# A recurrent layer with a gated residual: the gate's second layer in four steps instead of eight, and each later stage begun earlier

## The chip, the cores and the metric

The kernel runs on one core of one Trainium2 chip. The metric is the device time of one execution in microseconds; 3016.45 us is the median of three runs (3016.45, 3016.9 and 3013.8). The profile is that of one further execution.

## What is computed

64 sequences of 256 steps, 1024 wide, all in fp32. The first layer is a recurrence, and the second one adds its input to a gated reconstruction of it:

```python
xW  = einsum('ntd,dh->nth', x, Wx) + b
h_t = tanh(h_{t-1} @ Wh + xW_t)             # h_{-1} = cond
x1  = x + h
h   = silu(cond @ W1.T + b1)
gate = sigmoid(h @ W2.T + b2)               # one row per sequence
y   = x1 + (x1 + inverse_haar(gate * haar(x1)))
```

The gate is the same for all coefficients of a sequence, so the transform and its inverse cancel, and `y = x1 * (2 + gate)`. The kernel calls `2 + gate` its `factor`. It needs the two layers of the gate once, and before the first output is scaled.

## The kernel before

**The products.** `h @ Wh` has to be done step by step. It is 64 x 1024 x 1024 in fp32, done as one level of Strassen's scheme: seven products of half size (`strassen_product`, L212), each of 16 matmuls 128x32 x 128x128 on four strips of TensorE. `x Wx` doesn't wait for the recurrence. It is done for two steps at a time, 128 rows, a "pair" n holding steps 2n and 2n + 1. To keep precision with the fast fp32r matmuls, x and Wx are split in pieces: 24 matmuls 128x128 x 128x512 go to each 512 columns, 8 to a bank `mixed` and 16 to a bank `main`, 48 in all (`XWork`, L291). The sum of both banks goes to DRAM and comes back in the layout of h (`sum_d`, `xw`). ACT copies the reloaded `xw` into the accumulators of the next step (`put`, `put_part`).

**The stages.** There are four, and `ALONE`, `SWITCH` and `FIRST` say where they part.

- Single steps, t = 0 to `ALONE` - 1 (L526 to L602; `ALONE` = 12). After each h product comes half an x product: `XWork.first` after odd steps (`mixed`, and the first third of `main`), `XWork.second` after even ones. From t = 3 (`LATE`) on, each step also loads one of eight blocks of W2 (512 KB each, L588) and multiplies it with the gate's hidden layer `g1T` (`plain_product`, L229, 16 matmul records per block). This gate product stands last in the step, after the half x product. After the eighth block `gate_factor` (L499) makes `factor`. Pairs that are finished before `factor` is there are put aside in DRAM (`kept`, L597). At the end of a pair the x of the pair three further on is loaded (`load_x`).
- Pairs of steps, t = `ALONE` to `SWITCH` - 1 (`SWITCH` = 22). Two h products follow each other, in a form that works by quarters of h (L1080 to L1131), and then one whole x product (`beside_x`, `XWork.whole`). The first of these whole products comes ahead of step `ALONE`. `kept_pair` (L698) reads a pair that was put aside, scales it and stores it.
- Pairs after the switch (`beside_two`, kind "plain"; seven pair numbers lie between `SWITCH // S` and `FIRST`). The same 48 matmuls, but other buffers: x is loaded a second time by steps (`r`), and the slabs of the first stages are given up (`switch`, L726). In these pairs the weights for the last stage are formed (`make_forms`).
- Units of two pairs, from pair `FIRST` = 18 on (kinds "one" for even and "two" for odd n). Six of the eight row blocks of Wx are done as before; the last two are done by Strassen's scheme over two pairs. A unit has 54 + 39 = 93 matmuls of 512 columns where two plain pairs have 96.

**What sets the order.** TensorE's order is the order in which the program is written, everywhere. DVE's and ACT's order is written out in the start-up and from step `ALONE` on; in the single steps between, a scheduler chooses it, and that of POOL and SP as well. All transfers but one are issued by SP, in order, so an issue that waits holds back what stands behind it. In the stages from `ALONE` on, `not_ahead_of` (L644) lets the store of the sums wait for an instruction late in the h products. `slab` tiles (six buffers of 512 KB) hold x, the blocks of W2 and the pairs that are read again; a load waits until the last reader of an old slab is done.

`nc.tensor.addr_align(256, 60)` near the end of an x product (L360, L1009) pads TensorE's instructions, so that what follows stands at a given place within a block of 256.

Of the kernel before, what the change touches and what calls it, by code (L numbers as in the profile page):

```python
# [53 lines left out]
F32 = mybir.dt.float32  # L54
# [6 lines left out]
N, T, D = 64, 256, 1024  # L61
P = 128
R = 32
Q = P // R
B = D // P
# [5 lines left out]
S = 2  # L71
# [6 lines left out]
WARM = 6  # L78
LATE = 3
AHEAD = 2  # L80
ALONE = LATE + B + 1
RINGS = 1024
BLOCK = 256
PLACE = 60
SWITCH = 22
FIRST = SWITCH // S + 7
FULL = B - 2
EVEN = 16
# [3 lines left out]
def tile_cond_resid(  # L92
# [16 lines left out]
    nc = tc.nc  # L109
# [5 lines left out]
    dram = ctx.enter_context(tc.tile_pool(name="dram", bufs=2, space=bass.MemoryType.DRAM))  # L115
# [13 lines left out]
    def slab(name: str):  # L129
        return slabs.tile([P, D], F32, tag="slab", name=name)  # L130
# [91 lines left out]
    def plain_product(ps, vT, w, k: int, of=None, start: bool = True, stop: bool = True) -> None:  # L222

        for g in range(G):
            col = of(g) if of else (g * B + k) * R
            for q in range(Q):


                nc.tensor.matmul(  # L229
                    out=ps[q * R : (q + 1) * R, g * F : (g + 1) * F],  # L230
                    lhsT=vT[:, col : col + R],
                    rhs=w[:, q * F : (q + 1) * F],
                    start=start and k == 0 and g == 0,
                    stop=stop and k == B - 1,
                    skip_group_check=True,
                    tile_position=(0, q * R),
                )

    def strassen_sides(hT, t: int):
        a11, a12, a21, a22 = (hT[:, i * E : (i + 1) * E] for i in range(4))  # L240
        s = sums.tile([P, 4, E], F32, tag="s", name=f"s{t}")
        nc.vector.tensor_add(s[:, 0], a21, a22)
        nc.vector.tensor_sub(s[:, 2], a11, a21)
        nc.vector.tensor_sub(s[:, 1], s[:, 0], a11)
        nc.vector.tensor_sub(s[:, 3], a12, s[:, 1])
        return {1: a11, 2: a12, 3: s[:, 3], 4: a22, 5: s[:, 0], 6: s[:, 1], 7: s[:, 2]}
# [4 lines left out]
    def put(xw, t: int):  # L251

        acc = bank("acc", f"acc{t}")
        nc.scalar.copy(acc, flat(xw))
        return acc
# [30 lines left out]
    def bank(tag: str, name: str):  # L286
        return one_pool.tile([P, HALF], F32, tag=tag, name=name)
# [165 lines left out]
    acc, acc1, gate_ps = bank("acc", "acc0"), bank("m57", "acc1_raw"), bank("gate", "gate_ps1")  # L453
# [17 lines left out]
    def gate_block(k: int) -> None:  # L471
        plain_product(gate_ps, h0T, w1[k], k)

    for k in range(B):
        x_block(k)
        split_block(k)
        if k == 0:
            now = XWork(1)
# [20 lines left out]
    def gate_factor(z):  # L499

        nc.vector.tensor_add(z, gate_ps, z)
        nc.scalar.activation(z, z, AF.Sigmoid)
        factor = const.tile([P, W], F32, tag="factor", name="factor")
        nc.vector.transpose(factor, z)
        nc.vector.tensor_scalar_add(factor, factor, 2.0)
        return factor

    def blocks(v):
        return v[:].rearrange("p (g b m) -> p g b m", g=G, b=B)
# [5 lines left out]
    def of_step(x, s: int):  # L515
        return x[:].rearrange("p (b s g m) -> p s g b m", b=B, s=S, g=G)[:, s]
# [4 lines left out]
    h = work.tile([P, W], F32, tag="h", bufs=1, name="h0")  # L521
    nc.vector.tensor_add(h, acc, b_n)


    kept, again, factor = [], [], None
    for t in range(ALONE):  # L526
        i, s = divmod(t, S)
        if s == 0 and t:
            xw = xw_next
        if t:  # L530
            h = h_product(acc, sides, t)
        hT = work.tile([P, W], F32, tag="hT", name=f"hT{t}")
        nc.scalar.activation(h, h, AF.Tanh)
        nc.vector.transpose(hT, h)
        sides = strassen_sides(hT, t)
        if t == 0:
            acc = bank("acc", "acc1")
            nc.vector.tensor_add(acc, acc1, b_n)
            for k in range(2, B):
                if k == B - 1:  # L540
                    for j in range(4):
                        gate_block(j)
                now.block(k)
            now.take_mixed()
            for k in range(4, B - 2):
                gate_block(k)
            later = XWork(2)
            wh_s = StrassenWeight(wh_raw)
            wh_s.first()
            wh_s.second()  # L550
            wh_s.third()
            wh_s.fourth()
            xw_next = now.finish()
            later.split()

        elif s == 0:
            acc = put(xw[1], t + 1)
            now.second()
            later = XWork(i + 2)
            later.split()  # L560
            xw_next = now.finish()
        if s == 1 and t + 1 < ALONE:
            now = later
            now.first()
            acc = put(xw_next[0], t + 1)

        if t == 1:
            in_order.close()
        if t == 2:
            g1T = gate_hidden(b1_n)  # L570
            b2_n = load_bias(b2, const, "h0T", "b2_n")


        x = pairs[i]
        if t == 0:
            hT0 = hT
        elif t == 1:

            for r, v in enumerate((hT0, hT)):
                tc.keep_in_program_order(nc.gpsimd.tensor_add(of_step(x, r), of_step(x, r), blocks(v)))  # L580
        elif t + 1 < ALONE:
            nc.gpsimd.tensor_add(of_step(x, s), of_step(x, s), blocks(hT))
        if LATE <= t < LATE + B:
            k = t - LATE
            if k == 0:
                gate_ps = bank("gate", "gate_ps2")
            w2 = slab(f"w2_{k}")
            nc.sync.dma_start(out=w2, in_=w2T[k])  # L588
            plain_product(gate_ps, g1T, w2, k)
            if k == B - 1:  # L590
                factor = gate_factor(b2_n)
        if t + 1 == ALONE:
            break
        if factor is not None:
            scale(x, s)
        elif s == S - 1:
            kept.append(dram.tile([P, D], F32, tag="kept", bufs=(LATE + B) // S, name=f"kept{i}"))  # L597
            nc.sync.dma_start(out=kept[i], in_=x)
        if s == S - 1:
            del pairs[i]  # L600
        if s == S - 1 or t + 2 == ALONE:
            load_x(i + 3)  # L602
# [20 lines left out]
    )  # L623
    xws = {ALONE // S: xw_next}

# [15 lines left out]
        v = x_step(t)  # L641
        nc.vector.tensor_add(v, v, blocks(hT))

    def not_ahead_of(dma, ins) -> None:  # L644
        tc.add_manual_dep(
            dma.ins,
            ins.ins.name,
            mybir.DependencyInfo(mybir.DependencyClass.Sync, mybir.DependencyReason.DATA),
            reason="transfers stay out of the products of h",
        )  # L650

    def store_y(i: int) -> None:
        nc.sync.dma_start(out=yT[i], in_=pairs.pop(i))

# [16 lines left out]
    def beside_x(t: int, later, now, scaled: list, mark):  # L671


        if later:
            d, dma = later.store()
            not_ahead_of(dma, mark)
        load_next()
        if later:
            xws[later.i] = later.reload(d, True)
        now.whole(True)  # L680
        residual(t, hT)
        for r in scaled:
            scale(pairs[r // S], r % S)
        now.take_mixed()
        if mark:
            accs[:] = [put_part(t + 1, j) for j in range(3)]
        nxt = XWork(now.i + 1)
        nxt.difference()
        nxt.low()
        now.finish_half(0)  # L690
        now.finish_half(1)
        kept_pair()
        store_done(t)
        return now, nxt

    again = []
# [22 lines left out]
    def store_step(t: int) -> None:  # L719
        nc.sync.dma_start(out=yS[t - SWITCH], in_=steps.pop(t))  # L720

    def load_step(t: int):
        steps[t] = new["pool"].tile([P, W], F32, tag="r", bufs=3, name=f"r{t}")
        return nc.sync.dma_start(out=steps[t], in_=xS[t - SWITCH])

# [119 lines left out]
    def beside_two(t: int, now, mark):  # L845
# [4 lines left out]
        n = now.i  # L850
        start_of = t + 1 == SWITCH
        kind = "plain" if n < FIRST else "one" if n % 2 == 0 else "two"
# [152 lines left out]
        for k, (out, lhs, rhs, start) in enumerate(todo):  # L1005
            for do in at.get(k, []):
                do()
            if k == len(todo) - 2 or kind == "two" and k == len(todo) - 2 - EVEN:
                nc.tensor.addr_align(BLOCK, PLACE - (3 * EVEN if k < len(todo) - 2 else 0))  # L1009
            if k == 1 and kind == "plain" and i in (SWITCH // S + 2, SWITCH // S + 3):  # L1010
                next(jobs[0])
# [11 lines left out]
        if kind == "plain":  # L1023
            jobs[0] = jobs[0] or make_forms()
            next(jobs[0], None) if i not in (SWITCH // S + 2, SWITCH // S + 3) else None
        if with_next:
# [23 lines left out]
    for t in range(ALONE, T):  # L1050
        i, s = divmod(t, S)
# [6 lines left out]
        h = work.tile([P, W], F32, tag="h", bufs=1, name=f"h{t}")  # L1058
        hT = None if final else work.tile([P, W], F32, tag="hT", name=f"hT{t}")
# [46 lines left out]
        mark = nc.scalar.copy(u, m16)  # L1106
# [80 lines left out]
```

## Time and profile before

| | us |
|---|---|
| median of three runs | 3016.45 |
| the profiled execution's own time | 3014.26 |
| its span, first to last instruction | 3012.5 |
| TensorE busy (matmuls) | 2999.2 |
| DVE busy | 2210.5 |
| POOL busy | 967.1 |
| ACT busy | 913.8 |

In the span, step 3 (the first one with a gate block) has its h product at 71.27, the single steps end at 181.88 with the start of the first whole x product, the pairs of steps run from 193.03, the h product after the switch begins at 310.36, and the first unit's x product at 443.67.

How to read the lines that follow later: in a timeline the first column is the start in us from the span's start, the second the time from the start of the first to the end of the last instruction of the merged group, then engine, source line, operation, output <- inputs, shapes, count. Matmuls are pipelined, and a group's end overlaps the start of the next one, so the length of a piece is taken as the difference of two starts. A bracket at the end tells how long the engine idled ahead of the group and what ended it; "issue" means that nothing in the profile was waited for. `m`, `m_h`, `main_h` and `acc` are banks of the h products, `gate_ps` that of the gate. The queue q8 carries TensorE's instructions, q1 the kernel's transfers.

### The profile page before, as it was taken

The page shows a single profiled execution, that of the slowest core. Times are in us where ns is not written, and L with a number is a line of the kernel's source. Part 1 is how long each engine was busy: PE and PEld are TensorE (multiplying, and loading weights), DVE is VectorE, ACT ScalarE, POOL GpSimd, SP SyncE. Part 2 cuts the span into 40 slices and gives each one's busy share as a digit, 9 for nine tenths or more (in the row PEclk, how much of TensorE's full clock was granted, in tenths as well). Part 3 has the DMA queues.
Part 4 walks back from the last instruction along what each step waited for, and adds up shares of the span by engine and source line. Part 5 has one row for each costly group of instructions (what it writes and reads, how often), then busy time and mean ns, then how long its engine had stood idle before and what let it go on. Part 6 is the DMA issues. An engine that isn't in the chain of part 4 may idle for free.

```text
span 3012.5 us, 147059 instructions
## 1 busy us (share of the span) xinstructions
PE 2999.2 (100%) x63697; PEld 2674.8 (89%) x63697; DVE 2210.5 (73%) x5594; ACT 913.8 (30%) x2753; POOL 967.1 (32%) x800
## 2 busy tenths in 40 slices
PE   9999999999999999999999999999999999999999
PEld 6888888998898889988988889889988998899888
DVE  7555667777777777777777777777777777777776
ACT  3222232322333233223332232233332322333222
POOL 2233333333333333333333333333333323333331
PEclk9999999999999999999999999999999999999999
DMA  7334454444544544445445444454454444544543
GB/s 266 115 114 135 156 179 157 142 149 151 170 143 142 171 157 141 150 153 167 143 142 170 158 141 146 153 171 143 141 172 157 141 149 152 170 143 143 172 155 111
DMA packets 263546, 461.99 MB, mean 153 GB/s; under 512 B 30080, under 2 KB 103552, under 8 KB 262912
## 3 DMA queue, kind: packets, MB, share of 16 engines
q1 hardware_dynamic: 262768, 452.06, 46.6%
q8 instruction: 514, 8.42, 1.1%
q14 instruction: 120, 0.98, 0.1%
q10 hardware_dynamic: 144, 0.52, 0.0%
HBM read 313.00 MB, written 139.46 MB: 150 GB/s over the span
## 4 chain that ended last, share of the span: by engine, by line
PE 97%; DMA 1%; POOL 0%; SPq 0%; issue 0%; DVE 0%; ACT 0%; DVEq 0%; POOLq 0%
PE main L890 23%; PE acc L212 22%; PE m_h L212 15%; PE main_h L212 14%; PE mixed L890 12%; PE chain_main L890 3%; PE main L291 3%; PE chain_mixed L890 2%; PE mixed L291 1%; PE m L212 1%; PE acc L229 1%; DMA xw<-sum_r 0%; PE gate_ps L229 0%; DMA x<-xT 0%; SPq L793 0%; POOL sum L337 0%
## 5 line engine op out<-in xcount | busy, mean ns | idle before, releaser
L890 PE MATMUL main<-wx,x 128*128 128x512 f32 x3052 | 746.4, 389 | 0.0
L871 POOL TENSOR_TENSOR r<-r,factor 128x512 f32<-128x512 f32 x230 | 318.7, 1386 | 1282.7 <-DVE r L639 998.1
L890 PEld LDWEIGHTS main<-wx,x 128*128 128x128 f32 x3052 | 572.8, 188 | 119.2
L786 POOL TENSOR_TENSOR xw<-xw,b_h 128x512 f32<-128x512 f32 x230 | 384.9, 1680 | 328.5 <-DMA xw<-sum_r 275.3
L1063 ACT ACTIVATE h<-h 128x128 f32<-128x128 f32 x976 | 275.5, 306 | 522.8 <-DVE h L1089 312.8
L890 PE MATMUL mixed<-wx,x 128*128 128x512 f32 x1526 | 389.0, 399 | 0.0
L632 ACT COPY acc<-xw 128x128 f32<-128x128 f32 x726 | 184.9, 267 | 554.9 <-POOL xw L786 460.1
L890 PEld LDWEIGHTS mixed<-wx,x 128*128 128x128 f32 x1526 | 277.4, 188 | 76.5 <-issue 23.0
L1067 DVE STREAM_TRANSPOSE hT<-h 128x128 f32<-128x128 f32 x972 | 298.1, 307 | 41.6 <-ACT h L1063 39.5
L212 PE MATMUL acc<-t,hT 128*32 128x128 f32 x8160 | 270.8, 273 | 2.1 <-issue 1.2
L212 PE MATMUL acc<-wh,s 128*32 128x128 f32 x8160 | 271.4, 273 | 1.5 <-issue 1.5
L212 PE MATMUL acc<-wh,hT 128*32 128x128 f32 x8160 | 269.7, 273 | 0.0
L212 PE MATMUL m_h<-wh,hT 128*32 128x128 f32 x7808 | 261.0, 274 | 1.7 <-ACT u L1106 1.7
L212 PE MATMUL main_h<-t,s 128*32 128x128 f32 x7808 | 260.6, 273 | 0.6 <-issue 0.5
L212 PE MATMUL main_h<-wh,s 128*32 128x128 f32 x7808 | 258.8, 273 | 0.0
L212 PE MATMUL m_h<-t,s 128*32 128x128 f32 x7808 | 258.8, 273 | 0.0
L807 ACT ACTIVATE sum<-chain_mixed 128x512 f32<-128x512 f32 x220 | 131.7, 598 | 399.0 <-PE chain_mixed L890 343.7
L212 PEld LDWEIGHTS m_h<-wh,hT 128*32 128x32 f32 x7808 | 208.2, 110 | 44.6 <-DVE sum L810 18.3
L212 PEld LDWEIGHTS acc<-t,hT 128*32 128x32 f32 x8160 | 227.5, 110 | 5.2 <-ACT acc L632 1.9
L212 PEld LDWEIGHTS acc<-wh,s 128*32 128x32 f32 x8160 | 229.6, 110 | 1.8 <-issue 1.7
L212 PEld LDWEIGHTS acc<-wh,hT 128*32 128x32 f32 x8160 | 227.9, 110 | 0.3
L315 DVE TENSOR_TENSOR x<-x,x_high 128x1024 fp32r<-128x1024 f32 x127 | 215.7, 1699 | 9.3 <-PE main L291 9.3
(135 smaller groups left out, 4074.0 us busy)
## 6 DMA issues: line engine op xcount, KB each, us to landing
wx<-form SPq DMA_DIRECT2D x330, 256.0 KB, 6.3
x<-xT SPq DMA_DIRECT2D x128, 512.0 KB, 4.2
sum_r<-sum SPq DMA_DIRECT2D x468, 128.0 KB, 2.2
r<-xS SPq DMA_DIRECT2D x233, 256.0 KB, 5.8
yS<-r SPq DMA_DIRECT2D x233, 256.0 KB, 6.0
xw<-sum_r SPq DMA_DIRECT2D x232, 256.0 KB, 4.9
ahead<-xT SPq DMA_DIRECT2D x55, 128.0 KB, 4.6
sum_d<-sum SPq DMA_DIRECT2D x10, 512.0 KB, 2.9
```

The lines of the kernel that those rows point to most:

```text
L212: nc.tensor.matmul(out=out[q * R : (q + 1) * R], lhsT=a[:, k * R : (k + 1) * R], rhs=wh_s.sides[i][k][:, q], start=first and k == 0, stop= ...
L229: nc.tensor.matmul(out=ps[q * R : (q + 1) * R, g * F : (g + 1) * F], lhsT=vT[:, col : col + R], rhs=w[:, q * F : (q + 1) * F], start=start ...
L291: nc.tensor.matmul(out=acc[h], lhsT=v[:, k * P : (k + 1) * P], rhs=wx_s[k][which][:, h * HALF : (h + 1) * HALF], start=start and k == 0, s ...
L315: nc.vector.tensor_sub(self.x1, x, self.high)
L632: nc.scalar.copy(part, xws[t // S][t % S][:, j])
L786: nc.gpsimd.tensor_add(v, v, new["b"][:].unsqueeze(1).broadcast_to((P, G, F)))
L807: nc.scalar.activation(out, mixed, AF.Copy, scale=-1.0)
L871: nc.gpsimd.tensor_mul(steps[r], steps[r], factor)
L890: nc.tensor.matmul(out=out, lhsT=lhs, rhs=rhs, start=start, stop=stop, skip_group_check=True)
L1063: nc.scalar.activation(quad(h, j), quad(h, j), AF.Tanh)
L1067: nc.vector.transpose(quad(hT, j), quad(h, j))
```

## The change

The gate's second layer takes two blocks per step (`EACH = 2`), in steps 3 to 6. Its products are issued right after the h product and ahead of the half x product, and both loads of W2 of step t wait for the transpose of h of step t - 1. So `ALONE` goes from 12 to 8, `SWITCH` from 22 to 14 and `FIRST` from 18 to 14; three pairs are put aside instead of five. `not_ahead_of` is only moved up. The first whole x product is no longer padded.

```diff
+EACH = 2
-ALONE = LATE + B + 1
+ALONE = LATE + B // EACH + 1
-SWITCH = 22
+SWITCH = 14
 FIRST = SWITCH // S + 7
...
-    kept, again, factor = [], [], None
+    def not_ahead_of(dma, ins) -> None:
+        tc.add_manual_dep(
+            dma.ins,
+            ins.ins.name,
...
+        )
+
+    kept, again, factor, turned = [], [], None, []
     for t in range(ALONE):
...
-        nc.vector.transpose(hT, h)
+        turned.append(nc.vector.transpose(hT, h))
         sides = strassen_sides(hT, t)
+        for k in range((t - LATE) * EACH, (t - LATE + 1) * EACH) if LATE <= t < LATE + B // EACH else []:
+            if k == 0:
+                gate_ps = bank("gate", "gate_ps2")
+            w2 = slab(f"w2_{k}")
+            not_ahead_of(nc.sync.dma_start(out=w2, in_=w2T[k]), turned[t - 1])
+            plain_product(gate_ps, g1T, w2, k)
...
-        if LATE <= t < LATE + B:
-            k = t - LATE
-            if k == 0:
-                gate_ps = bank("gate", "gate_ps2")
-            w2 = slab(f"w2_{k}")
-            nc.sync.dma_start(out=w2, in_=w2T[k])
-            plain_product(gate_ps, g1T, w2, k)
-            if k == B - 1:
-                factor = gate_factor(b2_n)
+        if t == LATE + B // EACH - 1:
+            factor = gate_factor(b2_n)
...
-            kept.append(dram.tile([P, D], F32, tag="kept", bufs=(LATE + B) // S, name=f"kept{i}"))
+            kept.append(dram.tile([P, D], F32, tag="kept", bufs=(LATE + B // EACH) // S, name=f"kept{i}"))
...
-        now.whole(True)
+        now.whole(mark is not None)
```

More of the change, by code (lines that the diff above doesn't have):

```diff
@@ L522, in tile_cond_resid @@
     nc.vector.tensor_add(h, acc, b_n)
-    kept, again, factor = [], [], None
+    def not_ahead_of(dma, ins) -> None:
+        tc.add_manual_dep(
+            dma.ins,
+            ins.ins.name,
+            mybir.DependencyInfo(mybir.DependencyClass.Sync, mybir.DependencyReason.DATA),
+            reason="transfers stay out of the products of h",
+        )
+    kept, again, factor, turned = [], [], None, []
     for t in range(ALONE):
@@ L642, in residual @@
         nc.vector.tensor_add(v, v, blocks(hT))
[L644 to L650, printed above, removed]
     def store_y(i: int) -> None:
```

## The prediction

> **What bounds the kernel.** I read the page first: the busy table, the chain that ended last, and the queue table.
>
> ```profile
> span 3012.5 us, 147059 instructions
> PE 2999.2 (100%) x63697; PEld 2674.8 (89%) x63697; DVE 2210.5 (73%) x5594; ACT 913.8 (30%) x2753; POOL 967.1 (32%) x800
> ...
> q8 instruction: 514, 8.42, 1.1%
> ...
> PE 97%; DMA 1%; POOL 0%; SPq 0%; issue 0%; DVE 0%; ACT 0%; DVEq 0%; POOLq 0%
> ```
>
> TensorE is busy for the whole span and is 97% of the chain. So the time is a sum of TensorE pieces that follow each other, and an edit is worth what it takes out of, or puts into, that sum. POOL, DVE and ACT have room. Secondly I read TensorE's timeline to get the length of each piece. One single step (step 6, and the start of step 7):
>
> ```profile
> 111.56 1.06 PE L212 MATMUL m<-wh,hT 128*32 128x128 f32 x32
> ...
> 117.78 5.78 PE L291 MATMUL main<-wx,x 128*128 128x512 f32 x24
> 123.49 1.07 PE L229 MATMUL gate_ps<-w,g1T 128*32 128x256 f32 x16
> 124.38 1.06 PE L212 MATMUL m<-wh,hT 128*32 128x128 f32 x32
> ```
>
> Differences of the first column: h product 117.78 - 111.56 = 6.22, half an x product 5.71, one gate block 0.89, in all 12.82 us. One pair of steps, in the stage after it, and one unit of two pairs, later:
>
> ```profile
> 216.49 1.08 PE L212 MATMUL m_h<-wh,hT 128*32 128x128 f32 x32
> ...
> 239.96 1.08 PE L212 MATMUL m_h<-wh,hT 128*32 128x128 f32 x32
> ...
> 549.48 1.08 PE L212 MATMUL m_h<-wh,hT 128*32 128x128 f32 x32
> ...
> 595.73 1.08 PE L212 MATMUL m_h<-wh,hT 128*32 128x128 f32 x32
> ```
>
> A pair is 23.47 us and a unit of two pairs 46.25 (the next one 46.26). The windows view of these stretches shows TensorE busy in all of them at a granted clock of 1.00. A plain pair after the switch is 23.47 too (336.30 to 359.77). Thirdly, the places where the pieces are longer than that. In step 4:
>
> ```profile
> 84.07 1.06 PE L212 MATMUL m<-wh,hT 128*32 128x128 f32 x32
> ...
> 88.44 0.61 PE L212 MATMUL acc<-t,hT 128*32 128x128 f32 x12
> 89.97 0.74 PE L212 MATMUL acc<-t,hT 128*32 128x128 f32 x18 [0.93 <-issue]
> ...
> 91.62 5.73 PE L291 MATMUL main<-wx,x 128*128 128x512 f32 x24
> ```
>
> Here the h product takes 7.55 us instead of 6.22, and TensorE waits for "issue", that is for no tile. In step 5 it takes 6.86. Steps 6 to 11 show none of it. What it waits for is its own instructions: counted in the built program (an fp32 matmul as two weight loads and two matmuls, padding included) TensorE has 131,665 instructions, 514.3 times 256, and q8 carried 514 packets of 16 KB. In an h product 448 instructions pass in 6.22 us, so 256 last 3.56 us. In step 4 a block's packet began at 87.03, took 1.24, and TensorE went on at 89.97; meanwhile the queue of SP had issued, in the middle of it, a block of w2 (84.23) and an x load (84.67), and the DMA moved 340 to 430 GB/s from 85.8 to 87.9.
>
> ```profile
> 84.23 0.35 SPq L588 DMA_DIRECT2D w<-w2T  x1
> 84.67 0.38 SPq L134 DMA_DIRECT2D x<-xT  x1
> 98.22 0.33 SPq L403 DMA_DIRECT2D sum_d<-sum  x1
> 98.64 0.38 SPq L588 DMA_DIRECT2D w<-w2T  x1
> ```
>
> So a stall needs two things: a block asked for early in an h product, and a data transfer under way just then.
>
> **The change, part by part.** (1) *Steps 8 to 11 become two pairs, and x products 5 and 6 whole ones.* Four steps without gate are 4 x (6.22 + 5.71) = 47.72; two pairs 2 x 23.47 = 46.94. Gain 0.8.
>
> (2) *Gate.* The count of matmuls stays. Eight pieces of 0.89 (7.1) become four of two blocks; a run of 32 gate matmuls in the start-up takes 43.30 to 45.05 = 1.75, so 7.0. Gain 0.1.
>
> (3) *Units from pair 14 instead of 18.* Pairs 14 to 17 cost 4 x 23.47 = 93.88 now and 2 x 46.25 = 92.50 as units. Gain 1.4. The built order agrees: 36 plain x matmuls less and 30 for the units more, 6 fewer, at 0.227 us each 1.36.
>
> (4) *The switch at step 14.* Pairs 7 to 10 go from whole products to plain ones, 23.47 against 23.47: nothing. The h product just after the switch shows 14.84 us against 12.36 (310.36 to 325.20; loads of 2.2 MB are issued from 307.43 on). The same transfers are issued in the same order at the new place, and the alignment puts the h product at place 64 of a block as before, so I carry these 2.5 us over unchanged, and likewise the 1.9 us of smaller stalls in the pieces from 359.77 to 503.01.
>
> (5) *Two pairs less are put aside and read again* (kept, again): DMA alone, nothing on TensorE.
>
> (6) *The w2 loads.* Their new wait for the transpose of the step before holds SP's queue. In step 2 hT is done at 67.97, where SP issued w2_0 at 66.90: 1.1 later. Queued behind it are w2_1, the load of x4, the store of the sums and the reload of xw4. The store waits for DVE till 72.2 anyhow; xw4 was consumed by ACT's copy at 81.17 and is needed by the second product of step 4 at 84.94 (85.8 in the new plan): 3.8 us of cover. x4 lands about 2 later than 72.9, but then the 76.2 of g1T comes first on DVE; y of step 3 moves from 76.19 to about 76.9, behind which lie 7.4 us of gate and x on TensorE. g1T is there at 76.26 and the first gate block is due at 77.52. The landing of w2 took 3.4 to 5.8 us here: issued at 68.5, w2_1 is there by 74.3, cover 3 us. In step 3 w2_2 and w2_3 go behind kept (81.50) at about 82, landed by 88 and due at 91.2. In step 4 w2_4, w2_5 and x5 wait for hT4 (about 94) and for the slabs that the gate of step 4 reads till 93. x5 went out at 84.67 and now goes at 95, landing by 100.5; DVE's mask of it stands ahead of y of step 5, due at 103: cover 2.5, and behind it the 7.4 of gate and x again. w2_7 follows kept2, which waits for POOL (1.4 us): issued by 109.5, due at 119.4. So I cost the waits at nothing; with its cover gone a late block costs what it is late, one for one, since TensorE takes its work in order.
>
> (7) *The stalls for instructions in the single steps.* Those of before, 1.33 in step 4 and 0.64 in step 5, go with their arrangement: 2.0. New ones come by the same rule. Each step now has 64 gate instructions, so the h products of steps 4 to 7 start at places 143, 192, 241 and 34 of a block. Without stalls they start at 84.95, 98.6, 112.3 and 126.0. Step 4: the block is asked for about 0.7 us into it, at 85.7, while kept, w2_2 and w2_3 (1.6 MB, at the 340 GB/s of that row 4.7 us) move from 82.7 to 87.4: late, but less than before; estimate 0.6. Step 5: asked for at its very start, 98.6, with w2_4, w2_5 and x5 moving until 99.9; estimate 0.4. Step 6: its boundary lies in the x product ahead; none. Step 7: asked for at 128.2 with the sum's store; about none. The pair after them is not aligned any more, but starts at place 68 where the alignment makes 64. Bounds: nothing at the one end (six of eight gate steps had none), at the other each of four steps 1.33 and the first pair 2.47, in all 7.8. I take 1.0, nearest to the rows of steps 4 and 5.
>
> The Trainium skill, in "Runtime: NRT & Kernel Launch", section "Instruction fetch mechanics", also says that code comes in 16 KiB blocks of 256 instructions, and that crossing a block costs little and is mostly hidden. The rows agree on the size; on the cost they show 0.93 us of idle in one crossing. By the page part (7) would add nothing and the change would give 4.2; by the rows it gives 3.2.
>
> **Sum.** 0.8 + 0.1 + 1.4 + 2.0 - 1.0 = 3.3 us off the profiled execution: span 3012.5 to 3009.2, its own time 3014.26 (1.8 outside the span) to 3011.0. The median of the runs shown, 3016.45, is 2.2 above that execution, and three runs spread from 3013.8 to 3016.9. I put the median after at 3016.45 - 3.3 = 3013.2, or 0.11% less. About 0.2%, 6 us, is what can be told from no change here.
>
> **Rivals.** *A, faster.* The stalls after the switch (2.5 + 1.9) hang on how a burst of loads meets a block's request. If the shorter stage before it shifts them apart, 4.4 more goes: 3008.8, with no new stalls in the single steps 3007.8. For it: they are as accidental as those of step 4. Against: same order of transfers, same places in the blocks.
>
> *B, a little slower.* More data per step means a stall in each of four h products, and one at the first pair: 7.8 instead of 1.0, 3020.0. For it: 1 MB of w2 in each step is released just ahead of the next h product. Against: six steps of before took transfers without a stall.
>
> *C, slower by over 0.2%.* A pair of w2 blocks comes after its gate products are due, and TensorE stands there in each of four steps. It decides from the point where a block lands over 9 us after its issue (due 91.2, issue 82), and to cost more than the 3.3 gained plus 6 it must be 2.3 late every time: 3022.5 and more. For it: kept, two w2 and x now stand in one row on the queue. Against: 5.8 us was the longest landing of eight.
>
> *D, it does not do what it says*: excluded, since the built order shows the matmuls gone and the same 131,665 places, padding taken in.
>
> **Chances.** Forecast (3011 to 3016) 0.60; A 0.17; B 0.16; C 0.07. Faster by over 0.2% (below 3010.4): most of A and the edge of the forecast by the spread of runs, 0.16. Slower by over 0.2%: C, 0.07. Within: 0.77. The range leaves out C, the upper end of B and the lowest of A: 3008.8 to 3018.5.
>
> **What would show it.** TensorE's timeline: gate pieces of 32 matmuls of 1.75 at steps 3 to 6 right behind the h product, with no idle ahead of them (else C); the h products of steps 4 to 7 near 6.22, those of 4 and 5 up to 0.6 over; the first pair product at about 143 us; pairs at 23.47, units of 46.25 from pair 14, the long h product after the switch again near 14.8. If that one is 12.4, A; if steps 6 and 7 or the first pair show "issue", B. Wrong altogether if units or pairs have another length.

## The result, and the profile after

The changed kernel takes 3029.34 us (median of six runs, 3027.13 to 3030.56), the kernel before 3016.42 in the runs beside it: a ratio of 1.0045, with a 95% interval of 1.0034 to 1.0055. It is 13 us slower, where I had forecast 3 us less. The profiled execution took 3029.44 us, with a span of 3027.6.

The same rows of the page, of the changed kernel:

```profile
span 3027.6 us, 147439 instructions
PE 3001.3 (99%) x63691; PEld 2678.0 (88%) x63691; DVE 2223.1 (73%) x5654; ACT 917.9 (30%) x2777; POOL 983.4 (32%) x806
...
q8 instruction: 515, 8.44, 1.1%
...
PE 97%; DMA 2%; issue 1%; POOL 0%; DVE 0%; SPq 0%; ACT 0%; DVEq 0%; POOLq 0%
```

TensorE has 6 matmuls less, and yet the span is 15.1 us longer, with 1% of the chain under "issue". The count of instructions rose by 380, and TensorE fetched 515 blocks instead of 514. The six matmuls gone are those of the change; something else was added to TensorE's queue.

The single steps are as forecast. TensorE's timeline of step 5 and the start of step 6:

```profile
99.50 1.08 PE L213 MATMUL m<-wh,hT 128*32 128x128 f32 x32
...
105.64 1.91 PE L230 MATMUL gate_ps<-w,g1T 128*32 128x256 f32 x32
107.47 3.92 PE L292 MATMUL mixed<-wx,x 128*128 128x512 f32 x16
...
113.14 1.08 PE L213 MATMUL m<-wh,hT 128*32 128x128 f32 x32
```

The h product and both gate blocks take 99.50 to 107.47, 7.97 us (6.22 + 1.75 was the sum), and no gate product waits for its weights. SP's queue shows the loads (second column: issue of the merged group):

```profile
67.91 0.83 SPq L549 DMA_DIRECT2D w<-w2T  x2
...
82.47 12.82 SPq L549 DMA_DIRECT2D w<-w2T  x4
95.39 1.57 SPq L135 DMA_DIRECT2D x<-xT  x1
```

W2 and x go out within 0.7 us of the times worked out (68, 82, 94 to 95). The loss stands later, in the second whole x product:

```profile
157.09 3.92 PE L292 MATMUL mixed<-wx,x 128*128 128x512 f32 x16
160.85 6.96 PE L292 MATMUL main<-wx,x 128*128 128x512 f32 x30
180.17 1.19 PE L292 MATMUL main<-wx,x 128*128 128x512 f32 x2 [12.36 <-issue]
181.29 1.94 PE L213 MATMUL m_h<-wh,hT 128*32 128x128 f32 x32
```

The product takes 24.20 us instead of 11.10. After 30 of its 32 `main` matmuls TensorE stands still for 12.36 us. That is the place of `addr_align`, two matmuls before the end. And the group behind it takes 1.94 us where it takes 1.08 elsewhere. The windows view of the idle stretch and the two after it (PE busy, other engines, then granted clock, DMA share, GB/s):

```profile
167.80:180.17 12.37, 0.01 (x1) 0.03 (x1) 0.00 (x0) 0.00 (x0) 2.47 (x2) 0.69 0.23 78
180.17:186.10 5.93, 5.93 (x94) 4.93 (x98) 0.69 (x1) 1.21 (x2) 0.00 (x0) 0.50 0.01 3
186.10:195.97 9.87, 9.87 (x365) 9.67 (x357) 6.48 (x26) 3.24 (x13) 1.29 (x1) 1.00 0.06 24
```

While it stands the granted clock falls, and the next 5.9 us run at 0.50. The h product takes 14.68 instead of 12.36. So this one place costs 13.1 + 2.3 = 15.4 us. What stands there is seen when the line of `addr_align` is asked for by itself, in the changed kernel (from 160 to 182 us):

```profile
L361 PEldq NOP  x224: 13/13/13, 163.6 to 180.1; - x112
```

The padding is 224 empty instructions, from 163.6 to 180.1. In the trace their starts are 70 or 71 ns apart for the most part and 74 on average, and never more than 0.23 us: they fill the idle stretch to its end without a break. The same question to the kernel before, over the whole span:

```profile
L360 PEldq NOP  x109: 13/13/13, 188.4 to 284.3; - x109
```

These are five paddings in whole products, 1 + 4 x 27: the first product had landed at place 60, or one short of it, and shows a single empty instruction.

### The profile page after: what moved, and what is told of

It is laid out like the page before. It is cut to its first block, busy times and chain, and to the rows that moved or that the text cites. A ratio compares the mean times of both kernels' runs of the same rounds, so it can differ in the third digit from the quotient of the medians.

```text
span 3027.6 us, 147439 instructions
## 1 busy us (share of the span) xinstructions
PE 3001.3 (99%) x63691; PEld 2678.0 (88%) x63691; DVE 2223.1 (73%) x5654; ACT 917.9 (30%) x2777; POOL 983.4 (32%) x806
## 4 chain that ended last, share of the span: by engine, by line
PE 97%; DMA 2%; issue 1%; POOL 0%; DVE 0%; SPq 0%; ACT 0%; DVEq 0%; POOLq 0%
PE main L890 24%; PE acc L213 22%; PE m_h L213 15%; PE main_h L213 14%; PE mixed L890 13%; PE chain_main L890 3%; PE chain_mixed L890 2%; PE main L292 2%; PE mixed L292 1%; PE m L213 1%; DMA xw<-sum_r 0%; DMA wh<-wh 0%; DMA h0T<-condT 0%; DMA w<-w1T 0%; PE gate_ps L230 0%
## 5 line engine op out<-in xcount | busy, mean ns | idle before, releaser
L890 PE MATMUL main<-wx,x 128*128 128x512 f32 x3156 | 771.9, 389 | 0.0
L871 POOL TENSOR_TENSOR r<-r,factor 128x512 f32<-128x512 f32 x238 | 330.0, 1387 | 1322.8 <-DVE r L647 1029.0
L890 PEld LDWEIGHTS main<-wx,x 128*128 128x128 f32 x3156 | 592.5, 188 | 122.9
L786 POOL TENSOR_TENSOR xw<-xw,b_h 128x512 f32<-128x512 f32 x238 | 415.9, 1755 | 332.5 <-DMA xw<-sum_r 283.4
L890 PE MATMUL mixed<-wx,x 128*128 128x512 f32 x1578 | 402.3, 399 | 0.0
L890 PEld LDWEIGHTS mixed<-wx,x 128*128 128x128 f32 x1578 | 287.0, 188 | 79.0 <-issue 23.8
L316 DVE TENSOR_TENSOR x<-x,x_high 128x1024 fp32r<-128x1024 f32 x127 | 227.1, 1788 | 5.4 <-PE main L292 5.2
```

What stands on the lines that cost most here:

```text
L316: nc.vector.tensor_sub(self.x1, x, self.high)
L786: nc.gpsimd.tensor_add(v, v, new["b"][:].unsqueeze(1).broadcast_to((P, G, F)))
L871: nc.gpsimd.tensor_mul(steps[r], steps[r], factor)
L890: nc.tensor.matmul(out=out, lhsT=lhs, rhs=rhs, start=start, stop=stop, skip_group_check=True)
```

## The experiments

**Theory 1**: the padding. In the changed kernel the second whole product comes to `addr_align` when it has passed place 60 of its block, so that nearly a whole block is filled up, at 71 ns per empty instruction. **Theory 2**, a rival: TensorE waits there for code behind transfers, as in step 4 of before. **Theory 3**: the two gate blocks per step and their loads push something late into that product.

### No whole product padded

```diff
-        now.whole(mark is not None)
+        now.whole(False)
```

> The changed kernel with no whole x product padded, so that the first padding comes in the first pair after the switch. Theory 1 (the padding itself: 224 empty instructions of 71 ns, of which TensorE's queued matmuls cover 4): the 12.4 us of idle in the second whole product and the 2.3 us of half clock behind it go, 15.4 us together; median 3029.3 - 15.4 = 3014, ratio to before 0.999, padding of about 22 instructions in the first pair after the switch, covered. Theory 2 (TensorE waits there for its instructions because transfers are in the way): the transfers stay, so the idle stays and the time is 3028 to 3030. Theory 3 (the two gate blocks per step and their loads push something late into that product): likewise 3028 to 3030.

Measured: 3011.21 us (11 runs), ratio to before 0.9985 (0.9976 to 0.9994). The idle and the half clock are gone; the second whole product and the h products behind it:

```profile
156.22:167.32 11.10, 11.10 (x52) 8.93 (x49) 6.58 (x13) 2.27 (x7) 5.15 (x3) 1.00 0.62 192
167.32:179.68 12.36, 12.36 (x449) 12.16 (x448) 7.17 (x27) 4.46 (x15) 3.82 (x3) 1.00 0.25 89
```

The transfers are there as before (192 GB/s here, 189 in the changed kernel up to its idle), and the gate work is unchanged. So theory 3 falls. Theory 2 falls with it: taking out the padding also moves the places of what follows, but the empty instructions ran through the idle stretch without a break, which leaves no room for a wait for code. Without the padding the change gives 4.5 us (1.8 to 7.2).

### Only the padding, in the kernel before

```diff
-        now.whole(True)
+        now.whole(True, PLACE if mark else PLACE - 4)
```

> The kernel before with one number changed: the first whole product is padded to place 56 instead of 60, which it has just passed. Nothing of the change is in it. Theory 1: about 253 empty instructions, 18.0 us, less the 4.2 that queued matmuls cover: 13.8 us of idle, and 2.3 for the half clock behind it; 3016.4 + 16 = 3032. Theories 2 and 3: no loads and no gate work have moved, so 3016, unchanged.

Measured: 3033.36 us, ratio 1.0053 (1.0038 to 1.0069). One number, moved by 4, costs 16 us (11 to 21):

```profile
185.10 6.96 PE L291 MATMUL main<-wx,x 128*128 128x512 f32 x30
206.50 1.19 PE L291 MATMUL main<-wx,x 128*128 128x512 f32 x2 [14.44 <-issue]
```

The line of `addr_align` shows the 253 empty instructions. Over the idle stretch the DMA moved 1 GB/s, so no transfer is in the way there:

```profile
192.00:206.50 14.50, 0.06 (x1) 0.03 (x1) 0.00 (x0) 0.00 (x0) 1.79 (x2) 0.68 0.01 1
```

### The first whole product padded too

```diff
-        now.whole(mark is not None)
+        now.whole(True)
```

> The changed kernel with the first whole product padded as well. Theory 1: the padding moves from the second whole product to the first, and is about 197 instructions there, 14.0 us, of which 4.2 are covered: idle of 9.8 instead of 12.4 at about 139 us, the second product padded with 27 at no cost; about 2 us less than the changed kernel, 3027. Theory 2: the idle stays at the second product, where the transfers are, 3029. Theory 3: as theory 2.

Measured: 3026.79 us, ratio 1.0034 (1.0022 to 1.0046). The idle moves to the first product and is shorter, as theory 1 has it:

```profile
136.71 6.96 PE L292 MATMUL main<-wx,x 128*128 128x512 f32 x30
154.03 1.19 PE L292 MATMUL main<-wx,x 128*128 128x512 f32 x2 [10.36 <-issue]
```

### Another dose, at another place

```diff
-            if k == len(todo) - 2 or kind == "two" and k == len(todo) - 2 - EVEN:
+            if kind == "plain":
+                if k == len(todo) - 2 and start_of:
+                    nc.tensor.addr_align(BLOCK, PLACE + 120)
+            elif k == len(todo) - 2 or kind == "two" and k == len(todo) - 2 - EVEN:
```

> As e1_no_padding, but in the first pair after the switch the padding goes to place 180 instead of 60, and the five plain pairs after it are not padded. Theory 1: 142 empty instructions of 71 ns, 10.1 us, less 4.2 that the queued matmuls cover: 5.9 us of idle in the x product at about 202 us, and some of half clock behind it (2 us if it is as after 12 us of idle, none if that needs a longer one); 3011.2 + 6 to 8 = 3017 to 3019. If the cost of padding were a fixed one of a passed block boundary (a rival within the theory), 15 us as in the changed kernel, 3026; if only a padding over one block's queue counted, 3011.

Measured: 3019.6 us, ratio 1.0019 (1.0010 to 1.0028), 6 us over before and some 10 over e1_no_padding, with an uncertainty of nearly 4 on that difference; the 6 to 8 that were expected lie within it.

```profile
206.64 6.96 PE L890 MATMUL main<-wx,x 128*128 128x512 f32 x30
219.70 1.19 PE L890 MATMUL main<-wx,x 128*128 128x512 f32 x2 [6.10 <-issue]
```

The four doses together, lengths from TensorE's timeline:

| empty instructions | at 71 ns each | added to the x product | added to the h product behind |
|---|---|---|---|
| 142 | 10.1 | 6.8 | 2.1 |
| 197 | 14.0 | 11.1 | 2.2 |
| 224 | 15.9 | 13.1 | 2.3 |
| 253 | 18.0 | 15.2 | 1.7 |

The last column counts against 12.36. For 142 that is the h product after the switch, which takes 14.26 in e1_no_padding with a wait of 1.44 for instructions; here that wait is absent, and the half clock stands in its place. So against e1_no_padding this h product costs 0.2.

The cost goes with the count. In all four the idle begins 4.2 us after the first empty instruction, so the matmuls that stand ahead of the padding cover its first 4.2 us (some 58 of the empty instructions), and all beyond that is idle: 6.10, 10.36, 12.36 and 14.44 us. The x product loses some 0.7 us more, since its last two matmuls run at half clock. The half clock is paid once, after 6 us of idle as well as after 14. It is no fixed price of a block boundary.

### The new wait of the W2 loads

```diff
-            not_ahead_of(nc.sync.dma_start(out=w2, in_=w2T[k]), turned[t - 1])
+            nc.sync.dma_start(out=w2, in_=w2T[k])
```

> As e1_no_padding, and the loads of W2 don't wait for the transpose of h of the step before. Theory 1 holds the wait for nearly worthless: within 2 us of e1_no_padding, with stalls of 0.5 to 3 us in the h products of steps 3 to 7 where the changed kernel has 1.7. If the wait on SP's queue is a cost by itself (a second theory of where the rest of the loss is), 2 to 4 us less than e1_no_padding.

Measured: 3012.14 us, ratio 0.9987 (0.9979 to 0.9996), beside e1_no_padding's 0.9985: no difference that can be told. From the h product of step 3 to that of step 8 it takes 71.9 us and e1_no_padding 72.3. The wait shows neither as a cost nor as a gain.

### The gate alone, and units from pair 18

Two parts by themselves. The first is the gate in four steps with the stages of before:

```diff
-ALONE = LATE + B // EACH + 1
+ALONE = LATE + B + 1
-SWITCH = 14
+SWITCH = 22
...
         if s == S - 1:
+            nc.sync.dma_start(out=yT[i], in_=x) if factor is not None else None
             del pairs[i]
```

> The gate's second layer in four steps ahead of the half x products, as in the change, but with the stages of the kernel before (steps alone to 11, switch at 22, units from 18); pairs 3 and 4 are then scaled and stored at once. The padding of the first whole product is 0 as before. By the prediction's parts (2) and (7): 0.1 + 2.0 less new stalls of about 1.5 for the single steps, so 0.6 us less than before, 3015.6. If the two blocks per step are a burden by themselves (theory 3), 2 us or more slower than before.

Measured: 3013.6 us, ratio 1.0000 (0.9991 to 1.0009). No burden, which speaks against theory 3 once more; a gain of 0.6 is too small to tell. In its timeline the first pair begins at 190.92, 2.1 us ahead of before.

The second is e1_no_padding with `FIRST = SWITCH // S + 11`:

> As e1_no_padding, but units of two pairs begin at pair 18 as in the kernel before; four more plain pairs. By the prediction's part (3) 1.4 us more than e1_no_padding, 3012.6, with units of 46.25 and plain pairs of 23.47 in the timeline. If earlier units are worth more than their matmuls, 3 us or more.

Measured: 3013.14 us, ratio 0.9999 (0.9990 to 1.0008), beside 0.9985 for e1_no_padding. That is 4 us of difference with an uncertainty of nearly as much, so it agrees with 1.4 and doesn't prove it. The timelines do: units are 46.25 and plain pairs 23.47 in both.

### The burst at the switch

```diff
-        nc.sync.dma_start(out=top, in_=wx[FULL])
+        not_ahead_of(nc.sync.dma_start(out=top, in_=wx[FULL]), late[0])
...
+        if t == SWITCH + 1:
+            late.append(mark)
+            next(jobs[0])
...
-            jobs[0] = jobs[0] or make_forms()
-            next(jobs[0], None) if i not in (SWITCH // S + 2, SWITCH // S + 3) else None
+            if start_of:
+                jobs[0] = make_forms()
+            elif i not in (SWITCH // S + 2, SWITCH // S + 3):
+                next(jobs[0], None)
```

> As e1_no_padding, but the loads of 1 MB for the weights' forms (top, low) are held until late in the first pair's h products after the switch, out of the burst of 2.2 MB at their start. If the stall of 1.9 to 2.5 us in that piece is a wait for instructions behind that burst: 0 to 1 us remain, and the later pieces are unchanged; 1 to 2 us less than e1_no_padding, 3009.5. If the stall comes from elsewhere (the switch of buffers), it stays at about 2, 3011.

Measured: 3010.62 us, ratio 0.9986 (0.9977 to 0.9995), the same as e1_no_padding within the interval. In the piece itself the expectation holds: without the hold TensorE waits for code inside the h product after the switch,

```profile
219.52 1.05 PE L213 MATMUL acc<-wh,s 128*32 128x128 f32 x30
222.00 0.38 PE L213 MATMUL acc<-wh,s 128*32 128x128 f32 x2 [1.44 <-issue]
```

and with it this wait is gone, with a short one for DVE in its place:

```profile
219.98 1.06 PE L213 MATMUL m_h<-wh,hT 128*32 128x128 f32 x32
221.30 1.08 PE L213 MATMUL acc<-t,hT 128*32 128x128 f32 x32 [0.27 <-DVE hT L1072]
```

The piece is 12.84 us instead of 14.26. The packet with the next block of code begins 5.5 us into the piece without the hold and 3.1 us with it. In the eight other profiles that have the burst (e5_padding_of_142 left out, which pads ahead of this piece), TensorE waits 0.82 to 2.26 us at this place. So that stall is one for instructions behind the burst. The 1.4 us are lost in the spread of the runs.

## Why the prediction was wrong

*What bounds the kernel* was right: the time is TensorE's sequence, and everything that moved it was in TensorE's own queue.

*Parts (1) to (3)* were right. Pairs took 23.47 and units 46.25. In e1_no_padding the first pair begins at 143.85 and lasts 23.47 as the others do; with two pairs added that is 190.8 for step 12, which before began at 193.03: 2.2 less, where parts (1), (2) and (7) give 0.8 + 0.1 + 2.0 - 1.0 = 1.9.

*Part (4)* was right in kind: the stall after the switch came back with 2.4 us (before 2.5), and 1.5 to 2 us follow it.

*Part (6)*, the waits of the loads at nothing: right, by the timeline and by e4_no_padding_no_wait.

*Part (7), new stalls of 1.0*: 1.6 in the changed kernel from step 3 to the first pair, 0.4 in e1_no_padding, within its bounds. But these stalls differ from execution to execution of the same instructions: e1_no_padding, e5_padding_of_142, e6_burst_later and e7_units_from_18 are alike up to the first pair, and take 72.3, 72.4, 72.0 and 74.0 us from step 3 to it. Likewise the 2.0 us of old stalls, read off one profile of before, are 1.2 in e2_before_padded, whose single steps are those of before. So the terms 2.0 and 1.0 were less certain than their digits, and that their difference came out is in part luck.

*The sum* of 3.3 for what the change means to do is borne out by e1_no_padding: 4.5 us, with an interval of 1.8 to 7.2. (Ahead of the sum I wrote 3.2 and 4.2 for the gain with and without new stalls; the terms give 3.3 and 4.3.)

The step that failed is the sentence in part (7), "The pair after them is not aligned any more, but starts at place 68 where the alignment makes 64", with rival D's "the same 131,665 places, padding taken in". I took the places in the blocks from a count of the built program and let the next padding follow from it: 23 instructions. The chip's profile shows 224, and I take one of them for `addr_align` itself; they cost the 15.4 us. My count of places stood 56 too low, and with 56 more the second product had passed place 60 by 33. Why the count was off was not found. The profile of before could have told me: my count gave a padding of 56 in its first whole product, and the row of L360 shows 109 empty instructions in all, four times 27 and one, so next to none there. And the fetched blocks, 515 against 514, go with 256 places more where my count had the same number. The padding of an alignment was a term that I never wrote into the sum. No range of mine held it, since the bounds of part (7) were for stalls by late code alone.

What remains of the 15.1 us of span: +15.4 from the padding, about -3.7 from the change and the pieces after the switch, +3.2 in the last piece, the h products from step 252 on (30.9 us against 27.7), and +0.2 behind it. There the last sums are read back; the issue rows of before and after, with the time to landing in us at the end:

```profile
last_sums<-sum_r SPq DMA_DIRECT2D x2, 256.0 KB, 3.6
```

```profile
last_sums<-sum_r SPq DMA_DIRECT2D x2, 256.0 KB, 4.8
```

In the ten profiles of this case this piece takes 27.0 to 31.7 us, short or long with every kind of edit (e1_no_padding 27.3, e6_burst_later 31.7). Nothing here ties it to the change. In the changed kernel TensorE idles 3.74 us in this piece, where it idles 1.68 in before, and then runs for 3.4 us at a granted clock of 0.50. Why the landing differs was not tried.

## What to carry to other kernels

An instruction that aligns code is a cost with a cliff: just short of its place it is free, just past it, it fills up a block, here with up to 253 empty instructions, 18 us, in one place. So whoever moves, adds or removes instructions ahead of one must count again where it falls, and check the count against the paddings of a profile (the row of its line), not against the listing alone. When a change whose pieces all came out as forecast is still slower, look first for instructions that only one engine's queue sees; here the fetched blocks (514 to 515) and one "issue" in the chain pointed at them.

## What the runs showed of the hardware

Empty instructions in TensorE's queue follow each other every 70 or 71 ns for the most part, 73 to 74 on average. Matmuls that stand ahead of them cover the first 4.2 us, some 58 of them. So the paddings of 25 to 27 in the pairs leave TensorE no idle.

The granted clock stayed at 1.00 through an idle of 1.44 us in e1_no_padding and 1.92 in the changed kernel, and fell to 0.50 in the idles of 6.10, 10.36, 12.36 and 14.44. The h product behind each of these took 1.7 to 2.3 us more than 12.36. The Trainium skill, in "TensorE: Matmul & The Clock Gate", section "Part 1: The HAM clock gate", puts the fall after one idle window of about 3.4 us. The six idles agree with that, but other rows of these runs don't: in e2_before_padded it fell 1.3 us after an idle of 2.26 us had ended, in the h products behind the switch (windows view, columns as above):

```profile
333.50:335.80 2.30, 0.05 (x3) 0.00 (x0) 1.14 (x6) 0.71 (x3) 0.00 (x0) 1.00 0.03 7
337.10:340.50 3.40, 3.40 (x74) 3.40 (x68) 2.78 (x8) 1.06 (x2) 1.66 (x1) 0.50 0.00 0
```

Near the end it fell in e5_padding_of_142 with idles of 1.75 and 0.33 us close to each other, and in e7_units_from_18 with 1.66 and 0.34; with 1.68 and 0.34 at the same place it stayed at 1.00 in the kernel before. So the length of an idle alone did not decide it here. What else did is not shown.
